# A second PSUM bank for the feed-forward's products while the last causal convolution runs

## The chip, the cores and the metric

The kernel runs on one core of a Trainium2 chip. The metric is the device time of one execution in microseconds (us). A core has engines with queues of their own: TensorE (PE) for matrix products, which go to PSUM, a memory of eight banks of 128 partitions by 512 fp32 numbers; VectorE (DVE) and ScalarE (ACT) for elementwise work; GpSimd (POOL) for some small operations and for issuing stores; SyncE (SP) for issuing loads. They run side by side and wait for one another through semaphores.

## The reference, cut to what matters

Two layers act on x of shape (4, 512, 128, 64): batch, time, frequency, channel. Layer 0 is, for each batch:

```python
x = x + attn                                   # a decayed scan over time, a few small products
x = x + gelu(conv over frequency of layernorm(x))
xn = layernorm(x)                              # over all 8192 = 128 * 64 features of a time step
to = causal depthwise conv of xn, 3 taps in time, plus time_b
to = layernorm(to) * time_ln_g + time_ln_b     # again over 8192 features
x = x + to
x = x + (gelu(x @ ffn_W1 + ffn_b1) @ ffn_W2 + ffn_b2)
```

Layer 1 replaces the sequence by its moving average plus a spectral filter of what is left. The change lies in layer 0, in the last three steps, and layer 1 begins when layer 0 has been written.

## The kernel before

Features lie on partitions and time (512 steps) on the free axis. The 8192 features of a batch are 64 columns of 128 features by 512 steps; two columns make a tile of 128 x 1024, so there are 32 tiles. Each stage is a Python generator that emits work for one batch and yields often. `in_turn` runs two generators side by side by written shares and leads, so that PE's order is the order in which the code emits matmuls (`manual_schedule` pins TensorE alone). The order on DVE, ACT and the other queues is set by the framework's list scheduler, except where `keep_in_program_order` pins an instruction. The framework also places the semaphores, from which tile an instruction reads or writes.

The stage around the change is the pairing in the list of `in_turn` that holds `F` of batch 2 beside `C` and `O` of batch 3:

- **Causal convolution** (`convolve_time`, `normed`, `tapped`), batch 3, one tile per step k. SP loads the tile. DVE normalises it in two passes (L608 multiplies, L611 subtracts). ACT writes the *base*, centre tap and bias, into a tile z (L616, two per tile, four buffers). DVE adds the other two taps (L620, four per tile). POOL mends the first two steps and issues the store (L626, L627). ACT squares the result (L667, two buffers). Two steps later PE adds tile and square into running sums: `add_up` (L251), four matmuls of the program, called a *sum* here. Its bank `st` is the first half of a two-bank tile "a" of the pool `ps_a`; nothing uses the second half meanwhile. After the last sum `finish` copies `st` out.
- **Feed-forward** (`feed_forward`), batch 2, one column per step c. `widen(c)` makes 256 hidden features (L718, into the two-bank tiles "m" and "c"), and ACT applies Gelu (L722, `mid`). `narrow(c - 1)` multiplies back to 128 features (L729, called a *narrow*) into `pa`, the only bank of the pool `ps_p`. DVE adds bias and residual to it and so empties the bank (L734, tile `x4t`, called an *exit*). `store(c - 2)` transposes the result on PE (L743) into another bank, ACT copies it out (L750, L752), and POOL issues the write. Every second step DVE prepares the residual of a later tile (L686, L687, L698), with ACT's scaling between (L695).

A trace shows each of the program's fp32 matmuls as two, except the transposes. The order within one step on PE is widen, narrow, store, and a step of the other generator may follow: its sum. What the page calls `pa<-mid` are narrows, `a<-z` and `a<-sq` sums, `pt<-ident,x4t` stores.

PSUM is full: two banks each for "a", "c" and "m", one each for "s" and "p".

Of the kernel before, what the change touches and what calls it, by code (L numbers as in the profile page):

```python
# [10 lines left out]
F32 = mybir.dt.float32  # L11
# [5 lines left out]
P = 128  # L17
# [5 lines left out]
SL = 512  # L23
# [56 lines left out]
def layer0(ctx, tc, dram, x, xt, vecs, wkvr, wo, wdec, wconv, fbias, w1, fb1, w2, fb2, x4):  # L80
# [5 lines left out]
    B = x.shape[0]  # L86
# [11 lines left out]
    ps_a = ctx.enter_context(tc.tile_pool(name="ps_a", bufs=1, space=PSUM))  # L98
# [3 lines left out]
    ps_p = ctx.enter_context(tc.tile_pool(name="ps_p", bufs=1, space=PSUM))  # L102

    def two(pool, tag):
        return pool.tile([P, 2, SL], F32, tag=tag, name=tag)
# [140 lines left out]
    def add_up(st, i, pair, squares, first, last):  # L246

        for j in range(2):
            for k, src in ((0, pair), (1, squares)):
                q = 2 * j + k  # L250
                nc.tensor.matmul(  # L251
                    st[32 * q : 32 * q + 32, :], lhsT=ones, rhs=src[:, j, :],
                    start=first, stop=last,
                )

    def finish(st, bank, tag):

        s_sb = rowp.tile([P, SL], F32, tag="s", name="s_sb")
        nc.scalar.copy(s_sb, st)
        yield CHAIN  # L260
        pm = bank()
        for t in range(NT):
            nc.tensor.matmul(
                pm[:, 2 * t : 2 * t + 2], lhsT=s_sb[:, t * P : (t + 1) * P], rhs=pick,
                start=True, stop=True,
            )
        me = tiny.tile([P, NT, 2], F32, tag=f"me{tag}", name="me")
        nc.vector.tensor_copy(me.rearrange("p t k -> p (t k)"), pm[:, 0 : 2 * NT])  # L268
        return me[:, :, 0], me[:, :, 1]

    def moments(mean, square, tag):

        var, rs, mrs = cols(f"var{tag}"), cols(f"rs{tag}"), cols(f"mrs{tag}")
        nc.vector.tensor_tensor(var, mean, mean, ALU.mult)
        nc.vector.tensor_tensor(var, square, var, ALU.subtract)
        rsqrt(rs, var)
        nc.vector.tensor_tensor(mrs, mean, rs, ALU.mult)
        return rs, mrs

    def rows(bank, a, b, names):  # L280
        both = rowp.tile([P, 2, SL], F32, tag=names, name=names)
        for k, col in enumerate((a, b)):
            pb = bank()
            spread(pb, col)
            nc.scalar.copy(both[:, k, :], pb)
            yield CHAIN
        return both[:, 0, :], both[:, 1, :]
# [9 lines left out]
    def spare(tag, n):  # L297
        return fr.tile([P, 2, n], F32, tag=tag, name=tag, bufs={"z": 4, "wx": 2}.get(tag, 3))
# [16 lines left out]
    ahead = {}  # L315
    begin = {}
    free_s = [True]
    held = [False]
    unscanned = [True]

# [278 lines left out]
    def fetch(tag, src, b, i):  # L599
        t = bk.tile([P, 2, SL], F32, tag=tag, name=tag, bufs=3 if tag == "kx" else 2)  # L600
        nc.sync.dma_start(t, src[b][2 * i : 2 * i + 2].rearrange("c p t -> p c t"))
        return t


    def normed(b, i, x2, xr, rb, mb, pinned=False):

        nc.sync.dma_start(x2, x2d[b][2 * i : 2 * i + 2].rearrange("c p t -> p c t"))
        first = nc.vector.tensor_tensor(xr, x2, pair_of(rb), ALU.mult)  # L608
        if pinned:
            tc.keep_in_program_order(first)  # L610
        nc.vector.tensor_tensor(xr, xr, pair_of(mb), ALU.subtract)  # L611
# [29 lines left out]
    def convolve_time(b):  # L641
        bank = of_a if b == B - 1 else of_p
        made = AHEAD if b in ahead else 0
        moment = carried.pop(b)
        if made:
            rb, mb = ahead.pop(b)
        else:
            rb, mb = yield from rows(bank, *moment, "rm" if b == B - 1 else "rm3")
        st = bank()
        waiting, added = [], 0  # L650
        n = NPR - made
        for k in range(n + 2):
            while waiting and waiting[0][0] == k - 2:
                add_up(st, 0, *waiting.pop(0)[1:], added == 0, added == NPR - 1)
                added += 1
            if k < n:
                if b == B - 1:

                    x2, xr, to, sq = spare("xp", SL), spare("x1", SL), spare("z", SL), two(bk, "sq")
                else:  # L660
                    x2 = bk.tile([P, 2, SL], F32, tag="kx", name="x2", bufs=3)
                    xr, to = two(bk, "kd"), bk.tile([P, 2, SL], F32, tag="k3", name="to", bufs=3)
                    sq = bk.tile([P, 2, SL], F32, tag="sq4", name="sq4", bufs=2)

                normed(b, made + k, x2, xr, rb, mb, made > 0 and k < 4)
                tapped(b, made + k, xr, to)
                nc.scalar.activation(sq, to, AF.Square)  # L667
                waiting.append((k, to, sq))
                i = k * made // n
                if i != (k + 1) * made // n:  # L670

                    to = fetch("kh", tod, b, i)
                    sq = bk.tile([P, 2, SL], F32, tag="mid", name="sq5", bufs=4)
                    nc.scalar.activation(sq, to, AF.Square)
                    waiting.append((k, to, sq))
            yield 7.0 * (NPR + 2) / (n + 2)
        mean, sq = yield from finish(st, bank, 4)
        causal[b] = moments(mean, sq, 4)

# [29 lines left out]
    def feed_forward(b):  # L709
        x3s = opened.pop(b)  # L710
        mids, x4s, obs = {}, {}, {}

        def widen(c, m):
            x3 = x3s[c // 2][:, c % 2, :]
            pm = c_bank() if m else two(ps_m, "m")
            for h in range(2):
                hs = slice(h * H, (h + 1) * H)
                nc.tensor.matmul(  # L718
                    pm[:, h, :], lhsT=w1_sb[hs, m * P : (m + 1) * P], rhs=x3[hs, :], start=True, stop=True
                )  # L720
            mid = mids[c, m] = bk.tile([P, 2, SL], F32, tag="mid", name="mid", bufs=4)
            nc.scalar.activation(mid, pm, AF.Gelu_apprx_tanh, bias=fb1_sb[:, m : m + 1])  # L722

        def narrow(c):
            pa = ps_p.tile([P, SL], F32, tag="p", name="pa")
            for m in range(2):
                mid = mids.pop((c, m))
                for h in range(2):
                    nc.tensor.matmul(  # L729
                        pa[h * H : (h + 1) * H, :], lhsT=w2_sb[:, m, :], rhs=mid[:, h, :],  # L730
                        start=(m == 0), stop=(m == 1),
                    )
            x4t = x4s[c] = bk.tile([P, SL], F32, tag="x4t", name="x4t", bufs=3)
            nc.vector.scalar_tensor_tensor(x4t, pa, fb2_sb, x3s[c // 2][:, c % 2, :], ALU.add, ALU.add)  # L734
            if c % 2:
                x3s.pop(c // 2)

        def store(c):
            x4t = x4s.pop(c)
            pool, tag = (ps_s, "s") if free_s[0] else (ps_p, "p")  # L740
            pt = pool.tile([P, NT, P], F32, tag=tag, name="pt")
            for t in range(NT):
                nc.tensor.transpose(pt[:, t, :], x4t[:, t * P : (t + 1) * P], ident)  # L743
            s = c // 4
            if c % 4 == 0:
                obs[s] = bk.tile([P, NT, SL], F32, tag="ob", name="ob")
            o = obs[s][:, :, c % 4 * P : (c % 4 + 1) * P]
            if c // 2 % 2:
                for h in range(2):
                    nc.scalar.copy(o[:, :, halves[1 - h]], pt[:, :, halves[h]])  # L750
            else:
                nc.scalar.copy(o, pt)  # L752
            if c % 4 == 3:
                nc.gpsimd.dma_start(
                    x4[b][:, s * SL : (s + 1) * SL].rearrange("(t p) d -> p t d", p=P), obs.pop(s)
                )

        early = None
        for c in range(NCH + 2):
            if c < NCH:  # L760
                widen(c, 0)
                widen(c, 1)
            i = c // 2 + 2
            if i < NPR:
                if c % 2:
                    x3s[i] = add_residual(b, i, *coming)
                else:
                    coming = residual(b, i)
            if 0 < c <= NCH:
                narrow(c - 1)  # L770
            if c > 1:
                store(c - 2)
            if b + 2 < B and c > 4 and c % 2:
                early = early or convolve_ahead(b + 1)
                next(early, None)
            yield 4.5
# [364 lines left out]
```

## Time and profile before

| what | value |
|---|---|
| median of 3 runs | 3782.92 us |
| lowest and highest | 3777.52 and 3785.83 us |
| the profiled execution's own time | 3802.5 us |
| its span, first to last instruction | 3800.7 us |
| PE busy over the span | 96% |
| DVE busy over the span | 71% |
| ACT busy over the span | 46% |
| mean granted TensorE clock | 0.975 |

The profile is of one execution, which took 0.5% more than the median of the timed runs; durations are read from it, and sums are made against its own time. In its lines the engine comes first or after the line number, `out<-in` names the tiles, and `A <- B` in a list of waits means that A was held up by B, with the total in us, the number of times and the longest. "Busy" on PE is how long matmuls were in flight, not the array's load.

### The profile page before, as it was taken

What the parts mean: (1) busy time and instruction counts of PE and PEld (TensorE: products, weight loads), DVE (VectorE), ACT (ScalarE), POOL (GpSimd) and SP (SyncE); (2) the same over time, 40 slices, a digit from 0 to 9 for tenths busy, and PEclk for the clock granted to TensorE, in tenths of its full rate; (3) what the DMA queues carried; (4) which work ended last, traced back from release to release, by engine and by line L of the source; (5) the groups of instructions that cost most, each with busy time, mean ns of one, the idle gap of its engine ahead of it and who ended that gap; (6) DMA issues with size and microseconds to landing.
All of it is one profiled execution on the core that took longest, in us unless ns stands there. A gap on an engine that the chain in (4) does not pass through costs nothing. (4 is left out here: it accounts for less than half of the span.)

```text
span 3800.7 us, 44873 instructions
## 1 busy us (share of the span) xinstructions
PE 3636.3 (96%) x15945; PEld 1345.5 (35%) x15945; DVE 2683.6 (71%) x3498; ACT 1761.2 (46%) x2491; POOL 513.3 (14%) x782
## 2 busy tenths in 40 slices
PE   9989999999999999999999988999989999999998
PEld 4433322223333223333322322333322843327533
DVE  4445559976777896677789799755567277892677
ACT  0013336645656565566656678867744210142100
POOL 0000012210011221011122221100012000131001
PEclk9999989999999899999999999999999999999999
DMA  9867647786874788787478677545567478993687
GB/s 310 272 203 242 229 146 264 254 288 241 287 280 169 247 285 287 251 278 278 172 258 282 205 249 262 202 155 177 183 222 246 146 236 295 309 294 140 205 296 264
DMA packets 429175, 912.80 MB, mean 240 GB/s; under 512 B 33240, under 2 KB 83608, under 8 KB 424856
## 3 DMA queue, kind: packets, MB, share of 16 engines
q1 hardware_dynamic: 351024, 636.87, 49.7%
q0 software_dynamic: 75776, 271.62, 20.5%
q8 instruction: 127, 2.08, 0.2%
q10 hardware_dynamic: 2152, 1.45, 0.1%
q14 instruction: 96, 0.79, 0.1%
HBM read 641.31 MB, written 268.50 MB: 239 GB/s over the span
## 5 line engine op out<-in xcount | busy, mean ns | idle before, releaser
L729 PE MATMUL pa<-mid,w_sb 128*64 128x512 f32 x2048 | 500.2, 609 | 37.2 <-DVE x4t L734 37.2
L734 DVE SCALAR_TENSOR_TENSOR x4t<-pa,fb_sb,x 128x512 f32<-128x512 f32 x252 | 188.4, 748 | 345.7 <-PE pa L729 345.6
L722 ACT ACTIVATE mid<-m,fb_sb 128x1024 f32<-128x1024 f32 x256 | 285.1, 1114 | 280.5 <-PE m L718 280.2
L718 PE MATMUL m<-x,w_sb 64*128 64x512 f32 x1008 | 290.4, 649 | 0.4 <-ACT mid L722 0.4
L722 ACT ACTIVATE mid<-c,fb_sb 128x1024 f32<-128x1024 f32 x256 | 283.2, 1106 | 1.5 <-PE c L718 1.5
L718 PE MATMUL c<-x,w_sb 64*128 64x512 f32 x1008 | 263.4, 596 | 1.3 <-ACT mid L722 1.3
L729 PEld LDWEIGHTS pa<-mid,w_sb 128*64 128x64 f32 x2048 | 125.0, 136 | 379.9 <-issue 250.8
L406 PE MATMUL a<-xp,wx 128*128 128x512 f32 x512 | 240.7, 596 | 0.5 <-DVE me L268 0.5
L986 ACT COPY two<-a 128x512 f32<-128x512 f32 x64 | 37.5, 586 | 425.0 <-PE a L981 425.0
L1009 PE MATMUL b<-xin,avg_sb 128*128 128x512 f32 x512 | 230.8, 593 | 2.3 <-DVE xin L1015 2.3
L1015 DVE TENSOR_TENSOR xin<-b,pm 128x512 f32<-128x512 f32 x256 | 159.1, 684 | 95.6 <-PE b L1012 80.7
L567 ACT ACTIVATE sq<-x 128x1024 f32<-128x1024 f32 x128 | 135.0, 1054 | 180.5 <-DVE x L564 180.5
L620 DVE SCALAR_TENSOR_TENSOR to<-kd,vec,to 128x510 f32<-128x510 f32 (+1 forms) x272 | 197.8, 746 | 16.0 <-ACT to L616 10.4
L695 ACT ACTIVATE kd<-kd,vec 128x512 f32<-128x512 f32 x256 | 193.3, 809 | 3.1 <-DVE kd L687 3.1
L891 DVE COPY xf<-b 128x256 f32<-128x256 f32 x128 | 54.4, 425 | 185.3 <-PE b L955 173.2
L912 DVE TENSOR_TENSOR uv<-xin 128x1024 f32<-128x1024 f32 x128 | 155.4, 1227 | 39.4 <-DMA xin<-x 18.9
L251 PE MATMUL st<-x,ones 128*32 128x512 f32 x512 | 169.4, 611 | 13.3 <-DVE x L564 13.1
L743 PEld LDWEIGHTS pt<-ident,x4t 128*128 128x128 f32 x1024 | 107.7, 141 | 208.7 <-ACT mid L722 152.5
L528 DVE TENSOR_TENSOR x<-a,xp 128x1024 f32<-128x1024 f32 x128 | 156.2, 1220 | 33.6 <-PE a L526 31.1
L620 DVE SCALAR_TENSOR_TENSOR z<-x,vec,z 128x511 f32<-128x511 f32 x240 | 175.8, 745 | 5.7 <-ACT z L616 2.3
L526 PE MATMUL a<-rst,wo_sb 64*128 64x512 f32 x512 | 153.1, 672 | 27.2 <-DVE x L528 23.2
L743 PE MATMUL pt<-ident,x4t 128*128 128x128 f32 x1024 | 168.8, 288 | 1.5 <-ACT ob L750 1.5
(241 smaller groups left out, 6532.8 us busy)
## 6 DMA issues: line engine op xcount, KB each, us to landing
xp<-in_xt SPq DMA_DIRECT2D x256, 512.0 KB
xin<-x SPq DMA_DIRECT2D x128, 1024.0 KB
kh<-to SPq DMA_DIRECT2D x156, 512.0 KB
x<-x POOLq DMA_DIRECT2D x128, 512.0 KB, 4.4
kx<-x SPq DMA_DIRECT2D x128, 512.0 KB
x<-ob POOLq DMA_DIRECT2D x64, 1024.0 KB, 6.3
out<-xin POOLq DMA_DIRECT2D x64, 1024.0 KB, 7.1
x<-x SPq DMA_DIRECT2D x96, 512.0 KB
```

The costliest lines, as they stand in the source:

```text
L251: nc.tensor.matmul(st[32 * q : 32 * q + 32, :], lhsT=ones, rhs=src[:, j, :], start=first, stop=last,)
L406: nc.tensor.matmul(pa[:, k, :], lhsT=wq[:, j, k * P : (k + 1) * P], rhs=xp[:, j, :], start=first and j == 0, stop=last and j == 1,)
L528: nc.vector.tensor_tensor(x1, at, xp, ALU.add)
L620: tap = nc.vector.scalar_tensor_tensor(to[:, j, k:], xr[:, j, : SL - k], vec[:, w, c], to[:, j, k:], ALU.mult, ALU.add)
L695: tc.keep_in_program_order(nc.scalar.activation(d[:, j, :], d[:, j, :], AF.Identity, bias=vec[:, B4, c], scale=vec[:, G4, c]))
L718: nc.tensor.matmul(pm[:, h, :], lhsT=w1_sb[hs, m * P : (m + 1) * P], rhs=x3[hs, :], start=True, stop=True)
L722: nc.scalar.activation(mid, pm, AF.Gelu_apprx_tanh, bias=fb1_sb[:, m : m + 1])
L729: nc.tensor.matmul(pa[h * H : (h + 1) * H, :], lhsT=w2_sb[:, m, :], rhs=mid[:, h, :], start=(m == 0), stop=(m == 1),)
L734: nc.vector.scalar_tensor_tensor(x4t, pa, fb2_sb, x3s[c // 2][:, c % 2, :], ALU.add, ALU.add)
L743: nc.tensor.transpose(pt[:, t, :], x4t[:, t * P : (t + 1) * P], ident)
L1009: nc.tensor.matmul(po[j], lhsT=avg_sb[:, j, :], rhs=xin[:, j, :], start=True, stop=False)
L1015: nc.vector.tensor_tensor(by_n(xin[:, j, :]), by_n(po[j]), by_c(pm[j % 2][:, j // 2, :]), ALU.add)
```

## The change

While the causal convolution of the last batch runs, its generator takes both halves of the tile "a": the first for the running sums, as before, and the second is offered to the feed-forward through a one-element list. `narrow` writes odd columns there and even columns to the bank "p" as before. When the sums are complete the offer is withdrawn. Other batches are as they were, and no arithmetic changes.

```diff
+    second = [None]
...
-        st = bank()
+        if b == B - 1:
+
+            both = two(ps_a, "a")
+            st, second[0] = both[:, 0, :], both[:, 1, :]
+        else:
+            st = bank()
...
             yield 7.0 * (NPR + 2) / (n + 2)
+        second[0] = None
         mean, sq = yield from finish(st, bank, 4)
...
         def narrow(c):
-            pa = ps_p.tile([P, SL], F32, tag="p", name="pa")
+            pa = second[0] if c % 2 and second[0] is not None else ps_p.tile([P, SL], F32, tag="p", name="pa")
```

For batch 3 `bank` was already `of_a`, the first half of a two-bank tile "a", so the tile itself is not new; a part of it is used that was not.

## The prediction

> **What bounds the kernel now.** First the page's busy shares, then windows around the only stage the change touches, then its waits engine by engine, then the instructions one by one. The stage is the seventh pairing: feed-forward of batch 2 beside the causal convolution of batch 3, from about 2150 to 2477 us of the span.
>
> ```profile
> PE 3636.3 (96%) x15945; PEld 1345.5 (35%) x15945; DVE 2683.6 (71%) x3498; ACT 1761.2 (46%) x2491; POOL 513.3 (14%) x782
> ```
>
> Over the whole span TensorE (PE) is the bound. Windows (columns: length, then busy us and count of PE, its weight loads, DVE, ACT, POOL; clock, DMA share, GB/s) say otherwise here:
>
> ```profile
> 2160.00:2420.00 260.00, 226.40 (x1094) 74.91 (x1091) 256.23 (x289) 216.05 (x287) 54.79 (x69) 0.98 0.72 246
> 2420.00:2477.00 57.00, 56.45 (x282) 19.46 (x282) 34.05 (x37) 46.09 (x61) 5.85 (x8) 1.00 0.49 172
> ```
>
> For 260 us VectorE (DVE) is busy 98.5% and PE 87%; only the tail is PE's (99%). The waits in the first window, engine by engine:
>
> ```profile
> PE pa L729 <- DVE x4t L734: 31.9, 25, 3.9
> PE c L718 <- ACT mid L722: 1.3, 3, 0.6
> ...
> DVE z L620 <- issue: 1.8, 2, 1.3
> ...
> ACT z L616 <- PE a L251: 7.1, 17, 0.9
> ```
>
> PE loses 31.9 us waiting for the one bank of products; that is what a second bank addresses. But DVE, which it waits for, itself waits 1.8 us in all (1.34 us at 2214.8, 0.46 at 2261.7). The last line matters most: the base of a convolved tile (ACT, L616, tile z) waits for a sum on PE (L251), because its buffer, one of four, is free only when the sum that reads the tile of four steps earlier is done. Around one place (timeline: start, us, engine, what):
>
> ```profile
> 2304.35 0.62 PE L251 MATMUL a<-z,ones 128*32 128x512 f32 x1
> ...
> 2305.47 0.81 ACT L616 ACTIVATE z<-x,tb_all,vec 128x512 f32<-128x512 f32 x1 [0.42 <-PE a L251]
> ...
> 2306.42 0.74 DVE L734 SCALAR_TENSOR_TENSOR x4t<-pa,fb_sb,x 128x512 f32<-128x512 f32 x1
> 2307.08 2.97 DVE L620 SCALAR_TENSOR_TENSOR z<-x,vec,z 128x511 f32<-128x511 f32 x4
> ```
>
> The sum runs at 2304.35, the base follows at 2305.47, ends at 2306.28, and DVE takes up its taps at 2307.08, straight after the product's exit (x4t, L734), with 0.8 us to spare. This is c = 25; the pattern returns every eight columns, 45.2 us (2306.42, 2351.63, 2396.84).
>
> **What the Trainium skill says.** "Perfetto Trace Analysis", section Identifying Performance Opportunities: one generally gains by improving the most-contended engine. The trace agrees on who that is: DVE at 98.5%. "PSUM — Partial Sum Buffer", section PSUM bank collisions raise a hardware error: accesses are to be guarded by bank and quadrant, other banks not colliding. So the chip needs no guard between the two halves of the tile "a", two banks; no run here shows it yet. Same page, section Engine vs sequencer instructions: the queues of ScalarE and VectorE are strictly first in, first out. The trace agrees: ACT's base at 2305.47 holds the square and Gelus behind it. "TensorE: Matmul & The Clock Gate", section What's actually happening: the clock halves after an idle window of about 3.4 us that runs freely. The trace agrees loosely: of three waits above 2.5 us, those of 3.88 and 2.74 are followed by narrows of 3.68 and 2.62 us instead of 1.94, that of 3.15 is not.
>
> **The change part by part.** The order and the waits of the two programs as built differ as follows.
>
> Moved: the odd narrows of c = 3 to 55 write the second half of "a"; the PE order is otherwise the same. The 53 narrows of c = 3 to 55 lose their wait for the exit before, but each of these exits is still waited for: by 41 stores and 12 sums. The store of c-2 directly follows narrow c-1 and needs the same exit, so there the wait moves later by one narrow, 1.86 us (2301.90 to 2303.76), and no more.
>
> Removed: DVE's own 1.8 us of idle at most, since PE is less often late: -1.8 us. The 31.9 us of PE wait are not on the path: DVE has the same work. DVE's order is the same from c = 16 on, but for one normalising subtraction put ahead of a tap.
>
> Added: the 12 sums of 32 wait for an exit, namely those that directly follow the store behind an odd narrow (c = 7, 9, 15, 17, 23, 25, 31, 33, 39, 41, 47, 49). The exit reads the same tile "a" that the sum writes, so the framework's order by tile makes the sum wait although the banks differ. Behind the sum stand the rest of PE and, by the buffer above, the base on ACT with square and Gelus behind it; and DVE's taps wait for the base.
>
> Price where the taps follow the exit directly (c = 17, 25, 33, 41). From the exit's end: 0.06 us to PE (exit ends 2301.84, narrow starts 2301.90), sum 1.06 (2304.35 to 2305.41), 0.06 to ACT (2305.47), base 0.81, 0.06 to DVE by the same hop: 2.05. Today the taps start 0.08 before the exit's reported end (2307.08 against 2307.16). Stall 2.13. The third tap needs the second base, which ends 2.46 after the first begins (2305.47 to 2307.93); the taps would want it about 2.3 after: 0.15 more. So 2.3 us, four times: **+9.2**. DVE has nothing to hide it: it is the bound and takes its queue in order.
>
> Where two passes stand between (c = 15, 23, 31, 39: L608, L611, 1.14 + 1.23 us, taps 2.3 after the exit's end) the base at 2.05 comes in time: 0. No instruction or transfer is added, and SP and POOL issue as before. Withdrawing the offer costs nothing: the last odd exit (c = 55) is long done when the copy of the sums frees "a". Later narrows stay covered: after a held sum, widening (1.92) and narrow (1.86) end 4.85 us behind the exit, and DVE has 6.6 us or more before the next exit.
>
> Start (c = 7, 9): the sums hold ACT and PE 4 to 6 us, with little work of DVE behind: 0 to 2, I take **+0.8**, by the 0.3 us of margin at c = 9 and a slow clock after such waits.
>
> Tail: today PE runs free from 2420.55. Changed, exit 46 no longer waits (2.04 us there), but the sums behind 47 and 49 do: exit 47 ends 7.6 us after exit 45 (2420.5), 49 another 11.5 later (taps held 2.3, taps 2.9, residual passes, ACT's scaling), at 2439.6 before the stalls above; today that sum runs at 2438.11. **+1.6**, carried whole, since PE is the bound from there on (the feed-forward of batch 3 shows 200.00 of 200 us).
>
> Clock: in each eight columns PE now stands some 4.0 us at one sum and 2.7 at the next, instead of many waits under 2. The slow sum of the trace took 1.43 instead of 1.0 us (2210.23 to 2211.66); at worst double. Half of eight such places slow, at 0.3: **+1.2**, bounds 0 and 5.
>
> Sum: 9.2 - 1.8 + 0.8 + 1.6 + 1.2 = **+11 us**. The profiled execution took 3802.5 us (span 3800.7, 1.8 around it), which gives 3813.5; it was 0.5% slower than the median of the runs, 3782.92, to which I add the same 11: **3794 us**, +0.29%.
>
> **The rivals.** 0.2%, about 7.6 us, is what a measurement of this kernel can tell from no change.
>
> *The wait is harmless* (not slower): the exits come earlier than I think, so that held sums end before the base is wanted, and only DVE's idle goes. Place: c = 17, 25, 33, 41. It decides if the exit ends at least 2 us ahead of the taps; in today's order it ends in the very slot before them, which speaks against it. Price: -1.8, at most -4 with the 2.04 of the tail: 3779 to 3783. A weaker form, the stalls half as long or made good in the tail, gives +3 to +7: 3786 to 3790.
>
> *PE's waits were on the path*: the 31.9 us come back, 3751. Against it: DVE at 98.5%.
>
> *PE's clock decides*: the long stands slow PE each time, sums take 2.1 us, c = 15, 23, 31, 39 stall 0.7 too and narrows come late: +9.2 + 8 x 1.0 and some 3 more, about +20: 3803. For it: 2 of 3 long waits; against: even then PE has 13% of slack.
>
> That nothing changes is excluded: the order shows the new waits.
>
> **How the numbers follow.** My case (+7.6 to +16): 0.62. Clock case, above that: 0.12. Weak or harmless wait (-4 to +7.5, taken as no change): 0.23. Faster by over 0.2%: 0.03. The runs scatter by 8 us, so an effect of +8 may read as no change; I shift nothing for it. Slower 0.74, same 0.23, faster 0.03. Range 3784 to 3804: low end the weak form, high end the clock case; the likeliest alone 3790 to 3799.
>
> **What would show it.** Waits of PE for x4t before L729 (31.9 us) nearly gone in this stage; new ones of the store (L743 in today's lines) and of the sum (L251), each 4 and 2.7 us in turn; four idle spells of DVE of 2.1 to 2.4 us before taps, directly after an exit, put down to ACT's base; DVE busy of about 95 to 96% over the stage, with the same busy sum; the end of the stage's last sum some 10 us later; PE back to 100% afterwards, and nothing elsewhere. Wrong would be: no DVE idle after exits 17, 25, 33, 41 (then the time is 3783 or below), or PE at half clock through much of the stage (above 3800).

## The result and the profile after

The changed kernel took 3797.26 us in the median of 5 runs (3790.68 to 3802.32), the kernel before 3779.17 us in 5 runs beside it (3771.59 to 3785.83). The ratio is 1.0046, with a 95% interval of 1.0027 to 1.0066: slower by about 18 us. Its profiled execution took 3797.26 us with a span of 3795.5.

A difference of 18 us is hard to place in two spans that differ by chance elsewhere, so one measure is used from here on: the *stage*, from the first of the pick matmuls (L263) that end batch 2's convolution to the first of those that end batch 3's. In the kernel before, and then in the changed kernel (timeline of TensorE; start, us, engine, line, what):

```profile
2123.96 0.95 PE L263 MATMUL p<-pick,s_sb 128*128 128x2 f32 x8
...
2476.97 0.95 PE L263 MATMUL a<-pick,s_sb 128*128 128x2 f32 x8
```

```profile
2109.06 0.95 PE L263 MATMUL p<-pick,s_sb 128*128 128x2 f32 x8
...
2478.74 0.95 PE L263 MATMUL a<-pick,s_sb 128*128 128x2 f32 x8
```

That is 353.01 us before and 369.68 after. The stage is longer by 16.67 us, which is nearly all of the 18. The rest of the span (3795.5 - 369.7 = 3425.8 after, 3800.7 - 353.0 = 3447.7 before) differs by up to 23 us among the twelve profiles of this study, whatever the kernel does in the stage. The stage is steadier: two kernels in which no sum waits for an exit measure 349.43 and 349.34 below. Each figure of a stage comes from one profiled execution.

The windows of the changed kernel: the two stretches shown of before, although the stage begins 14.9 us earlier here (the first, moved by as much, gives the same share of VectorE), and one of the feed-forward that follows. The columns are length, then busy us and count of TensorE, its weight loads, VectorE, ScalarE and GpSimd, then clock, DMA share and GB/s:

```profile
2160.00:2420.00 260.00, 224.95 (x1044) 73.59 (x1036) 243.77 (x272) 202.62 (x270) 48.00 (x66) 0.93 0.69 236
2420.00:2477.00 57.00, 52.92 (x265) 18.35 (x266) 33.61 (x36) 43.74 (x60) 5.86 (x8) 1.00 0.45 158
2555.00:2755.00 200.00, 200.00 (x918) 72.88 (x914) 117.03 (x115) 154.48 (x207) 9.06 (x12) 1.00 0.52 180
```

VectorE's share in the first stretch fell from 98.5% to 243.77 / 260 = 93.8%, and TensorE's granted clock from 0.98 to 0.93. Afterwards TensorE is at 100% as before. The waits over the whole stage, first two of the kernel before, then those of the changed kernel, engine by engine:

```profile
PE pa L729 <- DVE x4t L734: 32.9, 26, 3.9
...
ACT z L616 <- PE a L251: 7.9, 19, 0.9
```

```profile
PE a L251 <- DVE x4t L741: 34.0, 12, 5.0
...
PE pt L750 <- DVE x4t L741: 2.1, 3, 0.7
...
PE pa L736 <- DVE x4t L741: 0.4, 1, 0.4
...
DVE x4t L741 <- PE pa L736: 18.9, 8, 5.0
DVE z L621 <- issue: 12.9, 7, 2.7
...
ACT z L617 <- PE a L251: 39.5, 21, 5.3
```

TensorE's wait for exits has not shrunk: over the whole stage 32.9 us in front of narrows became 34.0 us in front of twelve sums. The price is in the other lines. ScalarE's base waits 39.5 us for sums (7.9 before), and VectorE idles 12.9 us ahead of taps (1.8 before). Around c = 25, the place shown of the kernel before:

```profile
2296.06 0.74 DVE L741 SCALAR_TENSOR_TENSOR x4t<-a,fb_sb,x 128x512 f32<-128x512 f32 x1
2296.95 0.59 PE L251 MATMUL a<-z,ones 128*32 128x512 f32 x1 [1.49 <-DVE x4t L741]
2298.06 0.81 ACT L617 ACTIVATE z<-x,tb_all,vec 128x512 f32<-128x512 f32 x1 [1.97 <-PE a L251]
2298.96 3.14 DVE L621 SCALAR_TENSOR_TENSOR z<-x,vec,z 128x511 f32<-128x511 f32 x4 [2.16 <-issue]
```

Before, sum and base came ahead of the exit; now they come after it, one by one, and the taps start 2.16 us after the exit's end at 2296.80. The profile calls that wait "issue", which names no releaser; by the times it is the base, whose end (2298.87) comes just ahead. Where two normalising passes stand between exit and taps, at c = 39:

```profile
2381.59 1.03 PE L251 MATMUL a<-z,ones 128*32 128x512 f32 x1 [3.99 <-DVE x4t L741]
...
2384.47 3.13 DVE L621 SCALAR_TENSOR_TENSOR z<-x,vec,z 128x511 f32<-128x511 f32 x4 [0.63 <-ACT z L617]
```

TensorE had stood for 3.99 us, its first matmul took 1.03 instead of 0.59, and the taps came 0.63 late in spite of the two passes.

Comparing the starts of all exits, counted from the start of the stage, with those of the kernel before gives where the 16.67 us arise: 0.60 up to c = 15; 1.59 behind 15, 0.61 behind 23 and 1.08 and 1.42 behind 31 and 39, with 0.19 between these places, together 4.9; 1.69, 2.40, 2.99 and 2.39 behind c = 17, 25, 33 and 41, together 9.5; and 1.72 after c = 45.

### The profile page after: what moved, and what is told of

It reads as the page before. It is cut to its first block, busy times and chain, and to the rows that moved or that the text cites. A ratio compares the mean times of both kernels' runs of the same rounds, so it can differ in the third digit from the quotient of the medians.

```text
span 3795.5 us, 44906 instructions
## 1 busy us (share of the span) xinstructions
PE 3629.3 (96%) x15945; PEld 1344.4 (35%) x15945; DVE 2685.7 (71%) x3498; ACT 1761.3 (46%) x2491; POOL 508.1 (13%) x782
## 5 line engine op out<-in xcount | busy, mean ns | idle before, releaser
L736 PE MATMUL pa<-mid,w_sb 128*64 128x512 f32 x1832 | 444.4, 606 | 4.8 <-DVE x4t L741 4.8
L741 DVE SCALAR_TENSOR_TENSOR x4t<-pa,fb_sb,x 128x512 f32<-128x512 f32 x225 | 168.3, 748 | 344.0 <-PE pa L736 344.0
L736 PEld LDWEIGHTS pa<-mid,w_sb 128*64 128x64 f32 x1832 | 111.5, 136 | 311.9 <-issue 252.6
L621 DVE SCALAR_TENSOR_TENSOR z<-x,vec,z 128x511 f32<-128x511 f32 x240 | 176.5, 745 | 19.3 <-issue 12.9
L919 DVE TENSOR_TENSOR uv<-xin 128x1024 f32<-128x1024 f32 x128 | 156.1, 1230 | 33.2 <-PE a L928 17.2
L529 DVE TENSOR_TENSOR x<-a,xp 128x1024 f32<-128x1024 f32 x128 | 156.0, 1219 | 31.9 <-PE a L527 29.4
```

Source lines behind the costliest of these rows:

```text
L621: tap = nc.vector.scalar_tensor_tensor(to[:, j, k:], xr[:, j, : SL - k], vec[:, w, c], to[:, j, k:], ALU.mult, ALU.add)
L736: nc.tensor.matmul(pa[h * H : (h + 1) * H, :], lhsT=w2_sb[:, m, :], rhs=mid[:, h, :], start=(m == 0), stop=(m == 1),)
L919: nc.vector.tensor_tensor(t, xin[:, 0:2, :], xin[:, 2:4, :], op)
```

## The experiments

The theory: the sums' new wait for the exit, which exists only because sums and products share the tile "a", holds the base and so VectorE. The rivals are: (1) products in the second bank, or the waits moved to the stores, cost by themselves, by column; (2) VectorE's changed order is the cause; (3) every waiting sum costs alike; (4) z and its squares have too few buffers. All results in one table; "ratio" is to the kernel before on the same chip.

| run | stage, us | against 353.0 | ratio, 95% interval |
|---|---|---|---|
| changed kernel | 369.68 | +16.7 | 1.0046 (1.0027 to 1.0066) |
| e1_own_tile | 349.43 | -3.6 | 0.9997 (0.9979 to 1.0014) |
| e2_skip_twelve | 352.38 | -0.6 | 1.0007 (0.9995 to 1.0018) |
| e3_only_four | 364.60 | +11.6 | 1.0022 (1.0009 to 1.0035) |
| e4_other_four | 357.49 | +4.5 | 1.0003 (0.9987 to 1.0020) |
| e5_even | 372.62 | +19.6 | 1.0062 (1.0046 to 1.0078) |
| e6_more_buffers | 373.81 | +20.8 | 1.0055 (1.0035 to 1.0076) |
| e7_before_more_buffers | 358.64 | +5.6 | 1.0017 (1.0005 to 1.0028) |
| e8_four_filled | 367.15 | +14.1 | 1.0060 (1.0042 to 1.0078) |
| e9_four_filled_20 | 362.72 | +9.7 | 1.0037 (1.0024 to 1.0051) |
| e10_even_own_tile | 349.34 | -3.7 | 0.9987 (0.9974 to 1.0000) |

**The second bank as a tile of its own.** The pool of the two-bank tile is closed when the last convolution begins, and one with two one-bank tiles takes its place.

```diff
     def of_a():
+        if second[0] is not None:
+            return second[0].tile([P, SL], F32, tag="a", name="a")
         return two(ps_a, "a")[:, 0, :]
...
+        if b == B - 1:
+            for_a.close()
+            second[0] = for_a.enter_context(tc.tile_pool(name="ps_ab", bufs=1, space=PSUM))
+            free_b[0] = True
...
         def narrow(c):
-            pa = second[0] if c % 2 and second[0] is not None else ps_p.tile([P, SL], F32, tag="p", name="pa")
+            pool, tag = (second[0], "b") if c % 2 and free_b[0] else (ps_p, "p")
+            pa = pool.tile([P, SL], F32, tag=tag, name="pa")
```

> The second bank is a tile of its own: from the last convolution on, the two-bank tile a is given up and its two banks are handed out as two one-bank tiles, the sums in one, the products of the odd columns in the other. All products in front of the exit are in the same banks as in the changed kernel, all exits are waited for by the stores alone, and no sum waits for an exit. VectorE's order is that of the kernel before. Stage = from the pick matmuls that end the convolution before to those that end this one: 353.0 us before, 369.7 after. Theory (the sums' new wait, by way of the shared tile, holds the base and so VectorE): the stage falls back to 350 to 353.5 us and the time to -3 to +1 us of the kernel before. Rival 1 (the second bank's products, or the wait moved to the stores, cost by themselves): the stage stays above 362. Rival 2 (VectorE's changed order is what costs): as the theory here, but then the later runs that keep both must differ.

Measured: stage 349.43 us, 20.3 below the changed kernel and 3.6 below the kernel before. Waits in the stage, then the timeline around c = 25:

```profile
PE pt L754 <- DVE x4t L745: 18.2, 11, 3.7
...
DVE x4t L745 <- PE pa L740: 18.5, 8, 3.6
```

```profile
2290.24 0.62 PE L252 MATMUL a<-z,ones 128*32 128x512 f32 x1
...
2291.36 0.81 ACT L621 ACTIVATE z<-x,tb_all,vec 128x512 f32<-128x512 f32 x1 [0.42 <-PE a L252]
...
2294.11 0.74 DVE L745 SCALAR_TENSOR_TENSOR x4t<-pa,fb_sb,x 128x512 f32<-128x512 f32 x1
2294.77 2.97 DVE L625 SCALAR_TENSOR_TENSOR z<-x,vec,z 128x511 f32<-128x511 f32 x4
```

The base runs 2.75 us ahead of the exit instead of 2.0 behind it, and VectorE goes from exit to taps without a gap. Two banks for products and all waits in the stores: with these the stage is among the shortest of the table, so rival 1 falls. The 3.6 us are 1.8 by c = 45, VectorE's idle of the kernel before, and 1.8 in the tail. In the whole time they can't be told from nothing (0.9997).

**Twenty columns instead of thirty-two.**

```diff
-            pa = second[0] if c % 2 and second[0] is not None else ps_p.tile(...)
+            pa = second[0] if c % 2 and c not in {7, 9, 15, 17, 23, 25, 31, 33, 39, 41, 47, 49} and second[0] is not None else ps_p.tile(...)
```

> As the changed kernel, but the twelve odd columns whose products a sum follows directly (7, 9, 15, 17, 23, 25, 31, 33, 39, 41, 47, 49) keep the old bank; the other twenty odd columns use the second half. No sum has to wait for an exit, VectorE's order is that of the kernel before, and about half of the waits between successive columns are gone. Theory: stage 351 to 353.5 us, time -2 to +1 us of the kernel before. Rival 1 (cost by column in the second half): 20 of 32 columns, so about +10 us, stage 363.

Measured: 352.38 us, within the theory's range and far from rival 1's 363. The shared tile costs nothing as long as no sum directly follows an exit of it. Up to c = 33 the exits keep within 0.1 us of the kernel before; there one narrow after a wait of 2.52 us took 3.15 us and cost 1.1; the tail gained 1.8.

**Four sums, with and without cover.** Two runs, each with four of the columns alone in the second half.

```diff
+            pa = second[0] if c in {17, 25, 33, 41} and second[0] is not None else ps_p.tile(...)
...
+            pa = second[0] if c in {15, 23, 31, 39} and second[0] is not None else ps_p.tile(...)
```

> Only the products of columns 17, 25, 33 and 41 use the second half. Four sums wait for an exit, those after which VectorE's next work is the taps that hang on the base. Theory: each costs the 2.2 to 3.0 us by which the trace of the changed kernel loses ground there, together 9 to 11 us: stage 362 to 364. Rival (each of the twelve sums that wait costs alike, because TensorE stands and its clock falls): 4 of 12, +5.6 us, stage 358.6. Rival 1 (by column in the second half): 4 of 32, +2 us.

> Only the products of columns 15, 23, 31 and 39 use the second half. Four sums wait for an exit, each for some 4 us, but VectorE has two passes of 2 us in front of the taps that hang on the base. Theory: the stand itself is hidden; what the slow matmuls after it leave is 0.6 to 1.4 us each, 3 to 5 us together: stage 356 to 358. As predicted before the result: 0. Rival (each of the twelve costs alike): +5.6 us, stage 358.6.

Measured: 364.60 us, 0.6 above the theory's range, and 357.49 us, within it: +11.6 and +4.5 us for four waiting sums each, so rival 3 falls. In front of these sums TensorE waited 17.5 us in the one, 9.1 us in the other. By the exits, the first lost 2.6 behind c = 17 and 3.27 behind each of 25, 33 and 41. Its timeline at c = 25:

```profile
2302.10 0.74 DVE L741 SCALAR_TENSOR_TENSOR x4t<-a,fb_sb,x 128x512 f32<-128x512 f32 x1
...
2302.99 1.03 PE L251 MATMUL a<-z,ones 128*32 128x512 f32 x1 [4.70 <-DVE x4t L741]
...
2303.82 1.06 PE L251 MATMUL a<-z,ones 128*32 128x512 f32 x1
...
2305.87 3.13 DVE L621 SCALAR_TENSOR_TENSOR z<-x,vec,z 128x511 f32<-128x511 f32 x4 [3.03 <-issue]
```

The idle time is 3.03 us and not the 2.16 of the changed kernel. There TensorE came late to this sum, because it had stood at c = 23 already, waited only 1.49 us and ran at full clock; here it waited 4.70 us and ran slow. So the two groups don't simply add.

The second run was in its range, but partly for another reason than expected: the waits were 2.2 to 2.4 us and not 4. At c = 15 and at c = 23:

```profile
2228.82 1.03 PE L251 MATMUL a<-z,ones 128*32 128x512 f32 x1 [2.43 <-DVE x4t L741]
...
2231.70 3.14 DVE L621 SCALAR_TENSOR_TENSOR z<-x,vec,z 128x511 f32<-128x511 f32 x4 [0.63 <-ACT z L617]
...
2276.68 1.22 DVE L609 TENSOR_TENSOR x<-xp,rm 128x1024 f32<-128x1024 f32 x1
2276.91 0.59 PE L251 MATMUL a<-z,ones 128*32 128x512 f32 x1 [2.21 <-DVE x4t L741]
...
2277.93 1.22 DVE L612 TENSOR_TENSOR x<-x,rm 128x1024 f32<-128x1024 f32 x1
2279.07 2.98 DVE L621 SCALAR_TENSOR_TENSOR z<-x,vec,z 128x511 f32<-128x511 f32 x4
```

At the first the sum's matmuls take 1.03 us, the taps are 0.63 late and 2.3 us are lost before c = 18; at the second they take 0.59, the two passes cover the wait as predicted, and some 0.3 us are lost by c = 24. No wait of VectorE over 0.04 us lies in that stretch. What differs is the order: in the kernel before one tap stands between the two passes (L608 at 2294.80, L620 at 2295.93, L611 at 2296.59), while here, as in the changed kernel, the list scheduler has put the second pass directly behind the first at c = 15, 23, 31 and 39, and the same instructions follow one another less closely. So these 0.3 us belong to rival 2 and not to the wait. One more us of the 4.5 was lost behind c = 33, where this kernel has no waiting sum.

**Does the slow clock account for it?** The run with four columns again, with matmuls on the identity put where TensorE stood. They are added work, into a bank that nothing reads; 26 in the first of these runs, 20 in the second.

```diff
+            if c in {16, 24, 32, 40} and second[0] is not None:
+                pf = ps_p.tile([P, SL], F32, tag="p", name="pf")
+                for t in range(26):
+                    nc.tensor.matmul(
+                        pf[:, t % 4 * P : (t % 4 + 1) * P], lhsT=ident, rhs=ident, start=True, stop=True
+                    )
```

> As the run with columns 17, 25, 33 and 41 alone (stage 364.6 us), with 26 matmuls of 128x128 on the identity put ahead of each of the four waiting sums, into the old bank, which nothing reads: they fill some 4 us of the 4.7 us for which TensorE stood there. Theory of the slow clock (a stand of over 4 us is followed by matmuls at about 1.03 us in place of 0.6, and this is why each of the four costs 3.0 to 3.3 us here and 2.2 to 2.4 in the changed kernel): VectorE's idle time ahead of the taps falls from 3.0 to about 2.2 us, stage 361 to 362. Rival (the clock plays no part, the longer idle time has another cause): it stays at 3.0, stage 364 to 365, or more by what the added matmuls delay.

Measured: 367.15 us, worse than without and outside the theory's range; by the stage alone it would speak for the rival. At c = 25, where the exit ended at 2299.64:

```profile
2294.93 5.97 PE L754 MATMUL pf<-ident 128*128 128x128 f32 x52
2300.83 0.62 PE L251 MATMUL a<-z,ones 128*32 128x512 f32 x1
...
2302.85 3.13 DVE L621 SCALAR_TENSOR_TENSOR z<-x,vec,z 128x511 f32<-128x511 f32 x4 [3.20 <-issue]
```

The added matmuls overran the exit by 1.2 us, so the idle time says nothing; but from sum to taps there are 2.02 us instead of 2.88 (2302.99 to 2305.87). The run was repeated with fewer.

> As the run before it with added matmuls, with 20 in place of 26 of them: there each took 0.23 us, so that 26 lasted 5.9 us and ended some 1.0 us after the exit that the sum waits for; 20 should last 4.5 us and end just ahead of it. Theory of the slow clock: from the waiting sum to the taps 2.0 us as with 26 (2.9 without any), VectorE idle 2.2 us ahead of the taps of columns 25, 33 and 41 in place of 3.0 without the added matmuls, stage 361.5 to 363.5 us (364.6 without them, 367.2 with 26). Rival (the clock plays no part): 3.0 us, stage 364 to 365.

Measured: 362.72 us. At c = 25, with the same numbers at 33 and 41:

```profile
2289.24 4.63 PE L754 MATMUL pf<-ident 128*128 128x128 f32 x40
2294.10 0.59 PE L251 MATMUL a<-z,ones 128*32 128x512 f32 x1 [0.23 <-DVE x4t L741]
...
2296.11 3.14 DVE L621 SCALAR_TENSOR_TENSOR z<-x,vec,z 128x511 f32<-128x511 f32 x4 [2.16 <-issue]
```

The sum still waits for the exit, but TensorE doesn't stand for long, its matmuls are fast, and the idle time is 2.16 us in place of 3.03. Behind each of the three columns 2.40 us are lost, not 3.27. (At c = 17 the added matmuls overran the exit by 1.1 us and saved nothing.) The slow clock after a long wait is therefore a cost of its own, 0.87 us a place here. By whole time this run is not below the run without added matmuls (1.0037 against 1.0022, with intervals that overlap); 2 us are too little for that measure.

**The even columns.** More sums wait, but at other places of VectorE's list.

```diff
-            pa = second[0] if c % 2 and second[0] is not None else ps_p.tile(...)
+            pa = second[0] if c % 2 == 0 and second[0] is not None else ps_p.tile(...)
```

> The even columns use the second half instead of the odd ones. Twenty sums now wait for an exit, those that follow an even column, more than the twelve of the changed kernel; but on VectorE at least two passes lie between that exit and the taps that hang on the base, and in the run with a tile of its own these sums began after that exit anyway, or up to some 2.5 us ahead of it. The twelve sums that follow an odd column wait for none. Theory: what decides is where the waited-for exit lies, and nothing is held for long: stage 351 to 357 us (353.0 before, 369.7 in the changed kernel), likeliest 354; time within -2 to +4 us of the kernel before. Rival (each sum that waits costs alike, 16.7 / 12 = 1.4 us): 20 x 1.4 = +28 us, stage 381. Rival 1 (by column in the second half, 32 as before): +17 us, stage 370.

Measured: 372.62 us. The theory as it stood failed here. Waits in the stage, and the timeline behind c = 26:

```profile
PE a L251 <- DVE x4t L741: 42.7, 20, 6.5
...
DVE x4t L741 <- PE a L736: 21.2, 8, 3.6
DVE x4t L741 <- PE pa L736: 12.0, 9, 3.6
...
DVE z L621 <- ACT z L617: 2.5, 4, 0.6
```

```profile
2306.29 1.03 PE L251 MATMUL a<-z,ones 128*32 128x512 f32 x1 [6.53 <-DVE x4t L741]
...
2315.07 1.94 PE L736 MATMUL a<-mid,w_sb 128*64 128x512 f32 x8
...
2317.05 0.75 DVE L741 SCALAR_TENSOR_TENSOR x4t<-a,fb_sb,x 128x512 f32<-128x512 f32 x1 [1.70 <-PE a L736]
```

Two passes do cover the base, as expected: taps wait 2.5 us in all. But TensorE stood 6.53 us at one sum, with slow matmuls behind, and was then too late with the narrows, so that VectorE waited in front of exits: 33.2 us in place of 20.6. The expectation had put these sums at most 2.5 us ahead of their exits, because the run with a tile of its own had been read with the columns shifted: the sums that start 6.4 us ahead of an exit's end there follow even columns (26, 34, 42), not odd ones. And rival 1 named 370 here, close to the result, so the run alone would have spoken for it.

**The even columns in a tile of their own** decides that. The edit is that of the first run with `c % 2 == 0`; VectorE's list is that of the first run and of the kernel before.

> The even columns in the second bank, as in the run that used them (stage 372.6 us), but with the bank as a tile of its own, as in the first run. No sum waits for an exit. Theory (what cost 19.6 us there is again the wait of the sums, although it reached VectorE by another way: TensorE stood up to 6.5 us, and the exits waited for its later products): stage 349 to 351 us, as with the odd columns in a tile of their own. Rival 1 (products of even columns in the second bank cost by themselves): well above 353.

Measured: 349.34 us, as with the odd columns, so rival 1 falls here too: all 23.3 us of the difference from the even columns in the shared tile go with the sharing. The theory needs a second way for the sums' wait, TensorE's lateness with the next narrows. That this wait alone makes the 23.3 us is not shown: with the shared tile some 45 of VectorE's about 350 instructions in the stage stand elsewhere in its list, and no run with the even columns separates the order from the wait.

**More buffers.** Six for z and four for its squares, in the changed kernel and in the one before.

```diff
-                    x2, xr, to, sq = spare("xp", SL), spare("x1", SL), spare("z", SL), two(bk, "sq")
+                    x2, xr = spare("xp", SL), spare("x1", SL)
+                    to = bk.tile([P, 2, SL], F32, tag="sq4", name="to", bufs=2) if k % 3 == 2 else spare("z", SL)
+                    sq = two(bk, "x2" if k % 2 else "sq")
```

> The changed kernel with two more buffers for the outputs z of this convolution (six in place of four) and two more for their squares (four in place of two), in space that no later stage uses. Against it stands the next run, the kernel before with the same buffers. In the built program the base still waits for a sum, that of six outputs back in place of four: VectorE's list has moved two outputs ahead, so that the taps of columns 25, 33 and 41 again follow the exit directly; at column 17 other work now lies between. Theory: the buffers are spent on running ahead, and most of the loss stays: stage 10 to 15 us above that of the next run. Rival (too few buffers are the cause, and two more cure it): 0 to 3 us above.

> The kernel before with the same added buffers, six for z and four for the squares. Every theory: about the kernel before, stage 351 to 355 us; it serves as the ground for the run with the buffers in the changed kernel.

Measured: 373.81 and 358.64 us, 15.2 apart, a little above the theory's range; and the first is longer than the changed kernel with fewer buffers, so rival 4 falls. The list scheduler used the buffers to run ahead, and the same chain returned two tiles later. At c = 33 of the first:

```profile
2351.92 0.74 DVE L743 SCALAR_TENSOR_TENSOR x4t<-a,fb_sb,x 128x512 f32<-128x512 f32 x1
2355.69 3.13 DVE L621 SCALAR_TENSOR_TENSOR z<-x,vec,z 128x511 f32<-128x511 f32 x4 [3.02 <-issue]
```

The ground was missed: the buffers alone made the kernel before 5.6 us longer in the stage, where all theories had expected none. VectorE's list changed with them, not in the same way in the two runs, so the 15.2 us are a rough figure. In the kernel before with more buffers the loss arises between c = 16 and 22; why was not followed up.

**The order of VectorE's list** (rival 2) was not tried in a run of its own, but the run with columns 17, 25, 33 and 41 shows that it is not needed for the loss: there VectorE's instructions stand in the order of the kernel before, none moved, and the stage is 11.6 us longer. Where the order did change it has a part: some 0.3 us at c = 23 in the run with columns 15, 23, 31 and 39, where VectorE waits for nothing. What it costs in the changed kernel, at these four places and between c = 8 and 13, where more of the list is rearranged, was not separated.

## Why the prediction was right, and where it was not

The direction and the mechanism were right; the size was too small: +11 us were predicted, and +16.7 us were measured in the stage, +18 in the median. That the time itself came closer, 3794 us against 3797.26, is luck: the 11 had been added to 3782.92, and the kernel before took 3779.17 in the runs beside it. Of the 5.7 us that the sum fell short in the stage, 3.7 lie at the places with two passes and in the clock, 1.1 at the start, 0.7 where the taps follow the exit and 0.1 in the tail (VectorE's idle counted at its own places). Step by step:

- *Where the taps follow the exit directly, four times 2.3, +9.2.* Right. The changed kernel lost 9.5 net of the 0.46 us of idle that c = 17 had before; with full clock and nothing else changed it was 2.40 a place. The hop from exit to sum was 0.15 us and not 0.06 (2296.80 to 2296.95), and at c = 33 the clock added 0.6.
- *Where two passes stand between, 0.* This is the step that was too small, together with *Clock, +1.2*. These four places cost 4.9 us. With fast matmuls the zero is nearly right (0.3 at c = 23 in the run with these four columns, for the pass that was moved, which the prediction had seen and put at nothing); but in the changed kernel TensorE stood 3.99 to 4.02 us at all four, and at all four its matmuls were slow afterwards, at c = 23 only from the second half of the sum on. The prediction had priced the clock at 0.3 us for half of eight places; these four cost 0.6 to 1.6 each. How much of that is the clock rests on the two places compared in that run, 2.3 us with slow matmuls against 0.3 with fast ones; no run kept the clock up at these four.
- *Stands of 4.0 and 2.7 us in turn.* The first were right; the second were 1.4 to 2.0, since a stall at c = 23 makes TensorE later at c = 25. That kept three of these four sums fast and spared some 0.9 us at each.
- *VectorE's idle removed, -1.8.* Right in size, as the first run shows (-1.77 by c = 45), but in the changed kernel it is buried under the rest. The start, predicted +0.8 with 1.3 of these gained, came out at +0.6: 1.1 worse.
- *Tail, +1.6.* Measured 1.72. The other end was right too: without the sums' wait the tail gains 1.8, where 2.04 had been named.
- *TensorE's 31.9 us are not on the path.* Right: with 14.7 of the stage's 32.9 gone and no new wait of a sum, the stage shortened by 3.6, half of it VectorE's own idle and half the tail.

Of the rivals, the clock case (+20, by slow sums at every place and taps 0.7 late at c = 15, 23, 31 and 39) had its part right for those four places, where 0.63 was measured at c = 39; the outcome lies between it and the likeliest case. What the profile was to show came, except that VectorE fell to 93.8% and not 95 to 96%, that the stage ended 16.7 us later and not some 10, and that the idle was put down to "issue".

## What to carry to other kernels

When a free part of an existing tile is lent to other work, look in the built order for who now waits for whom: here the framework orders accesses by tile, so every user of one half can come to wait for users of the other. Give the lent part a tile of its own; that turned +16.7 us into -3.6 in the stage, though the gain is lost in the scatter of the whole time. A wait moved to another instruction is to be priced by what is queued behind that instruction, on its engine and, through its buffers, on the others, and more buffers don't cut such a chain if the scheduler spends them on running ahead.

## What the runs showed of the hardware

- In the stage, over all twelve profiles, each of the 25 waits of TensorE of 3.68 us and more was followed by a drop of its granted clock from 1.0 to 0.5, before it worked again or at most 1.1 us after. Waits of 1.96 to 3.65 us went either way: 2.43 us in front of a sum led to a drop and 2.21 us did so once in three, while 3.15 us in the kernel before and 3.65 us with twenty columns did not. Each drop lasted 3.4 or 6.8 us. A sum's first matmul after a drop took 1.03 us in place of 0.59.
- Useless matmuls in the gap kept the clock up, and shortened sum, base and hop to the taps from 2.88 to 2.01 us. They have to end ahead of what is waited for: 26 of them took 5.97 us, 0.23 each, of which a trace shows two records, while the four transposes of a store, of the same 128x128 and one record each, take 0.63 to 0.66 together.
